# A Gauss elimination beside a matrix exponential: new step, filled pauses, another order of loads

## The chip, the cores and the metric

The kernel runs on one core of a Trainium2 chip. The metric is device time in microseconds. Three runs of the kernel before took 2057.63, 2059.76 and 2062.48 us; their median, 2059.76, is the time before. A profile is one more execution: it took 2060.89 us, of which the trace spans 2059.2.

## The reference, cut to what matters

The input x has 8 batches of 512 tokens of 576 features. It is first rotated in a subspace of 64 dimensions, and then goes through one transformer block (layer norm, modulation, attention of 16 heads over the heads of each token, a projection, a wide layer and back).

```
U, _ = qr(P)                       # P is 576 x 64
v = silu(cond) @ W.T + b           # 2016 entries for each batch
A[iu, ju] = v; A[ju, iu] = -v
R = expm(A)                        # 64 x 64 for each batch
z = x @ U
x = x + (z @ R - z) @ U.T
ada = silu(cond) @ ada_w + ada_b   # shifts, scales and gates of the block
x = x + gate * attention(modulate(layernorm(x)))
x = x + gate * mlp(modulate(layernorm(x)))
```

So before the first token can enter the block, the kernel needs U (64 columns made orthogonal, with the signs that a Householder QR gives them), the exponential for that batch, and the shifts and scales.

## The kernel before, in words

**Two parts.** Everything up to L568 is the preparation, inside one block in which the order on four engines (PE, DVE, ACT, POOL) is the order in which the program writes the instructions; SP, which issues the loads, is ordered by a scheduler, which may also put later loads early. An engine takes its instructions in that order, so one that waits holds all behind it. After L568 comes the main part: 16 units of 256 tokens. Its opening (L1045 to L1098) is written out by hand: `rotation(b)` is a list of six pieces (`project_z` of each half, `rotate` of each tile of 128 tokens, L591 to L638), `feature_major` (L640) turns normed tokens and applies the shifts and scales, `qkv` (L671) makes six groups of 288 columns for one tile, ten matmul passes each, and `attention` (L700) runs on DVE. `next_sums` (L905) makes sums of weights on POOL.

**The Gauss steps.** The orthogonal basis comes from gram = P^T P (L271 to L274) by elimination. The tile w is 128 x 130. Rows 0 to 63 hold gram and beside it an identity; rows 64 to 127 hold the first 64 rows of P, from which the signs are found. `pivot(j)` (L276 to L315) is run 64 times. PE spreads row j over 64 partitions by a product with a column of the identity, four times: two halves of `row`, two of `own` (L283). DVE finds the sign of the leading element of the lower half (L294), adds half the scaled own row with that sign (q, L295), inverts q's first element (r, L300), makes one factor for each row (co, L301, with `below`, which is -1 under the diagonal and 0 above), and updates the window of w by one multiply-add (L304). ACT takes the root of the own leading element (hd, L308), DVE inverts it (inv, L309), and ACT scales the own row for the next step's q (rows2, L310). The next step's spreads read w.

**Beside the steps.** After each pivot, `next(side)` (L482) runs one piece of `beside` (L462): first the entries of A (`skew_entries`, five chunks of 4 concurrent column tiles of 504 columns, from the weights wr, 1 MB a chunk), which go to memory and come back in another layout (au), then the exponential (`expm`, a polynomial and 19 squarings of all eight matrices, each 16 passes of 64 x 64 on PE and one multiply-add on DVE), and three rounds of the modulation's weights (`ada_round`). At steps 48 to 52 the first 128 tokens are multiplied by P (L487).

**The tail, L495 to L568.** The scaled basis (mps, mn), one correction of its orthogonality (ups, u1, g2, fix, fps), the result m2; then ut (U in rows, L538), gz (rotation minus identity times U, L553), u (U in columns, ups2) and the rotation of the first 128 tokens from px: first_zT, first_rot (L563). Then their norm (L568), feature_major and the first group of qkv (L684).

Here is what the diff does to a step's core, before:

```
nc.vector.tensor_scalar(signs[:, j : j + 1], row[:, 0:1], 0.0, 0.5, ALU.is_ge, ALU.subtract)
nc.vector.scalar_tensor_tensor(q, rows2[j % 2][:, j : j + WIN], signs[:, j : j + 1], row, ALU.mult, ALU.add)
nc.vector.reciprocal(r[p], q[p, 0:1])
nc.vector.scalar_tensor_tensor(co[p], w[p, j : j + 1], r[p], below[p, j : j + 1], ALU.mult, ALU.mult)
```

Of the kernel before, what the change touches and what calls it, by code (L numbers as in the profile page):

```python
# [18 lines left out]
R = 64  # L19
# [30 lines left out]
def rotate_then_dit_block(  # L50
# [113 lines left out]
    with tc.manual_schedule(engines=engines), tc.tile_pool(name="prep", bufs=1) as prep, tc.tile_pool(  # L164
# [3 lines left out]
    ) as ps_row, tc.tile_pool(name="ps_g", bufs=2, space=PSUM) as ps_g, tc.tile_pool(  # L168
# [8 lines left out]
        nc.gpsimd.memset(w, 0.0)  # L177
        load_rows(ct, cond_t, 64)
        load_rows(m, p_in, 64)
        nc.sync.dma_start(out=w[R:128, 1 : R + 1], in_=p_in[0:R])  # L180
        nc.sync.dma_start(out=pt, in_=p_t)
# [11 lines left out]
        nc.gpsimd.tensor_copy(w[0:R, R : 2 * R], ident[0:R, 0:R])  # L193

        below = prep.tile([128, WIN], F32, tag="below", name="below")
        nc.gpsimd.memset(below, -1.0)
# [14 lines left out]
        inv = prep.tile([128, R], F32, tag="inv", name="inv")  # L211
# [18 lines left out]
        load_ada(0, (0,))  # L230

# [28 lines left out]
        nc.gpsimd.tensor_scalar(is_, i1, SIN_C[3], None, ALU.mult)  # L260
        tri = prep.tile([R, R], F32, tag="tri", name="tri")
# [7 lines left out]
        first_xt = xin.tile([128, D], F32, tag="xt", name="xt_0_0", bufs=2)  # L269
# [6 lines left out]
        def pivot(j):  # L276

            p = slice(0, R) if j == 0 else slice(0, 128)
            row = ps_row.tile([128, WIN], F32, tag="row", name=f"row_{j}")
            own = ps_g.tile([128, R], F32, tag="own", name=f"own_{j}")  # L280

            def spread(out_, k, rhs):
                nc.tensor.matmul(out_, lhsT=ident[:, k : k + 1].to_broadcast([128, R]), rhs=rhs, start=True, stop=True)  # L283

            if j:
                spread(row[R:128], j + R - 1, w[:, j : j + WIN])
            spread(row[0:R], j, w[:, j : j + WIN])
            for h in range(2):
                spread(own[h * R : h * R + R, 0 : R - j], j, w[:, j:R])
            q = step.tile([128, WIN], F32, tag="q", name=f"q_{j}")  # L290
            r = step.tile([128, 1], F32, tag="r", name=f"r_{j}")
            co = step.tile([128, 1], F32, tag="co", name=f"co_{j}")
            if j:
                nc.vector.tensor_scalar(signs[:, j : j + 1], row[:, 0:1], 0.0, 0.5, ALU.is_ge, ALU.subtract)  # L294
                nc.vector.scalar_tensor_tensor(  # L295
                    q, rows2[j % 2][:, j : j + WIN], signs[:, j : j + 1], row, ALU.mult, ALU.add
                )
            else:
                nc.vector.tensor_copy(q[p], row[p])
            nc.vector.reciprocal(r[p], q[p, 0:1])  # L300
            nc.vector.scalar_tensor_tensor(  # L301
                co[p], w[p, j : j + 1], r[p], below[p, j : j + 1], ALU.mult, ALU.mult
            )
            nc.vector.scalar_tensor_tensor(  # L304
                w[p, j + 1 : j + WIN], q[p, 1:WIN], co[p], w[p, j + 1 : j + WIN], ALU.mult, ALU.add
            )
            hd = step.tile([128, 1], F32, tag="hd", name=f"hd_{j}")
            nc.scalar.activation(hd, own[:, 0:1], AF.Sqrt, scale=0.25)  # L308
            nc.vector.reciprocal(inv[:, j : j + 1], hd)  # L309
            nc.scalar.activation(  # L310
                rows2[(j + 1) % 2][R:128, j + 1 : R + 1],
                own[R:128, 0 : R - j],
                AF.Identity,
                scale=inv[R:128, j : j + 1],
            )  # L315
# [15 lines left out]
        def skew_entries():  # L331
            n = NSKEW // 4
            ps = ps_m.tile([128, n], F32, tag="m", name="skew_ps")
            for c in range(NK):
                column_tiles(ps, wr, c, [t * n for t in range(4)], n)
                if c == NK - 1:
# [13 lines left out]
                yield  # L350
                yield

        def ada_round(g):
            ps = ps_m.tile([128, 320], F32, tag="m", name=f"ada_{g}")
            for c in range(NK):
                column_tiles(ps, aws[g], c, [0, 256, D, D + 256], 320)
                if c < NK - 1:
                    yield
            rows = prep.tile([128, 320], F32, tag=f"ada_rows{g}", name=f"ada_rows_{g}")
            nc.scalar.copy(rows, ps)  # L360
            if g == 0:
                load_ada(2)
                nc.sync.dma_start(out=first_xT, in_=x_t[0, :, :, 0:256].rearrange("c p s -> p c s"))
                nc.sync.dma_start(out=first_xt, in_=x[0, 0:128, :])
                nc.sync.dma_start(out=b1, in_=fc1_b)
# [4 lines left out]
            yield  # L370
# [16 lines left out]
            yield  # L387
# [11 lines left out]

        def expm():  # L400
# [3 lines left out]
            yield True  # L404
            nc.vector.tensor_tensor(a, au, products(au, i1, "at"), ALU.subtract)
            yield True
# [9 lines left out]
            yield True  # L416
            nc.scalar.copy(s2, products(s1, s1, "ss"))
            multiply_add(hc, s1, COS_C[4], ic)
            yield True
            nc.scalar.copy(s3, products(s1, s2, "sss"))  # L420
            multiply_add(hs, s1, SIN_C[4], is_)
            yield True
            multiply_add(hc, s2, COS_C[5], hc)
            yield False
            ps = products(s3, hc, "hc")
            multiply_add(hs, s2, SIN_C[5], hs)
            yield True
            ps2 = products(s3, hs, "hs")
            nc.vector.tensor_tensor(even, even, ps, ALU.add)
            yield True  # L430
            multiply_add(odd, s1, SIN_C[1], i1)
            yield False
# [6 lines left out]
            yield False  # L439
            nc.vector.tensor_tensor(odd, odd, ps2, ALU.add)  # L440
            yield False
            ps = products(a, odd, "sn")
            multiply_add(even, s2, COS_C[2], even)
            yield True
# [3 lines left out]
            yield False  # L448
            for k in range(N_SQUARINGS):
                e, f, e_next, f_next = es[k % 2], fs[k % 2], es[(k + 1) % 2], fs[(k + 1) % 2]  # L450
                if k < N_SQUARINGS - 1:
                    multiply_add(e_next, e, 2.0, products(f, e, f"pe_{k}"))
                    yield True
                multiply_add(f_next, f, 2.0, products(e, f, f"pf_{k}"))
                yield True
            nc.vector.tensor_tensor(fmi, f_next, nan.unsqueeze(2).to_broadcast([128, B // 2, R]), ALU.add)
# [5 lines left out]
        def beside():  # L462
            yield
            yield from skew_entries()
            yield
            yield
            yield
            rest = chained(ada_round(g) for g in range(3))
            for k, busy in enumerate(expm()):
                if not busy or k in (0, 2, 4):  # L470
                    next(rest, None)
                elif k > 16:
                    next(rest, None)
                yield
            for _ in rest:
                yield

        side = beside()
        xps = None
        for j in range(R):  # L480
            pivot(j)
            next(side, None)  # L482
            if 48 <= j < 48 + NK:
                c = j - 48
                if c == 0:
                    xps = ps_m.tile([R, 128], F32, tag="m", name="xps")
                nc.tensor.matmul(xps, lhsT=m[0 : KROWS[c], c], rhs=first_xT[0 : KROWS[c], c, 0:128], start=c == 0, stop=c == NK - 1)  # L487
                if c == NK - 1:
                    px = prep.tile([R, 128], F32, tag="px", name="px")
                    nc.scalar.copy(px, xps)  # L490

# [4 lines left out]
        diag, mt, mn = square("diag"), square("mt"), square("mn")  # L496
        nc.vector.scalar_tensor_tensor(diag, inv[0:R], 0.5, ident[0:R, 0:R], ALU.mult, ALU.mult)
        row = ps_row.tile([128, WIN], F32, tag="row", name="row_64")
        nc.tensor.matmul(row[:, 0:1], lhsT=one_row.to_broadcast([128, 128]), rhs=w[:, R : R + 1], start=True, stop=True)
        mps = ps_g.tile([R, R], F32, tag="own", name="mps")  # L500
        nc.tensor.matmul(mps, lhsT=w[0:R, R : 2 * R], rhs=diag, start=True, stop=True)
        nps = ps_g.tile([R, R], F32, tag="own", name="nps")
        nc.tensor.matmul(nps, lhsT=diag, rhs=w[0:R, R : 2 * R], start=True, stop=True)
        nc.vector.tensor_scalar(signs[:, R : R + 1], row[:, 0:1], 0.0, 0.5, ALU.is_ge, ALU.subtract)
        nc.scalar.copy(mn, mps)
# [4 lines left out]
        def u_rows(ps, of):  # L510
            for c, rows in enumerate(KROWS):
# [3 lines left out]
        sps = ps_row.tile([R, R], F32, tag="row", name="sps")  # L515
        nc.tensor.matmul(sps, lhsT=one_row.to_broadcast([128, R]), rhs=signs[:, 1:WIN], start=True, stop=True)
        nc.scalar.copy(u1[:, 0:4], ups[:, 0:4])
        nc.scalar.copy(u1[0:R, 4], ups[0:R, 4])
        upper, level, fix = square("upper"), square("level"), square("fix")
# [8 lines left out]
        fps = ps_g.tile([R, R], F32, tag="own", name="fps")  # L528
        nc.tensor.matmul(fps, lhsT=mt, rhs=fix, start=True, stop=True)
        nc.scalar.copy(m2, fps.unsqueeze(1).to_broadcast([R, 2, R]))  # L530
        for _ in side:
            pass
        first_zT = prep.tile([R, 128], F32, tag="first_zT", name="first_zT")
        zps = ps_row.tile([R, 128], F32, tag="row", name="first_z")
        nc.tensor.matmul(zps, lhsT=m2[:, 0], rhs=px, start=True, stop=True)
        for n in range(2):
            ps = ps_ex.tile([128, HALF], F32, tag="ex", name=f"ut_{n}")
            nc.tensor.matmul(  # L538
                ps,
                lhsT=m2.rearrange("p h i -> p (h i)"),  # L540
                rhs=pt[:, n * HALF : (n + 1) * HALF],
                start=True,
                stop=True,
            )
            if n == 0:
                nc.scalar.copy(ut[:, 0:HALF], ps)
                nc.vector.tensor_copy(first_zT, zps)
            else:
                nc.vector.tensor_copy(ut[:, HALF:D], ps)
        for n in range(2):  # L550
# [3 lines left out]
            if n == 0:  # L554
                nc.scalar.copy(gz[0:R, cols], ps)
            else:
                nc.vector.tensor_copy(gz[0:R, cols], ps)
        ups = ps_m.tile([128, NK, R], F32, tag="m", name="ups2")
        u_rows(ups, m2[:, 0])
        for n in range(2):  # L560
            cols = slice(n * HALF, (n + 1) * HALF)
            ps = ps_ex.tile([128, HALF], F32, tag="ex", name=f"first_rot_{n}")
            nc.tensor.matmul(ps, lhsT=first_zT, rhs=gz[0:R, cols], start=True, stop=True)  # L563
# [645 lines left out]
```

## Time and profile before

| what | value |
|---|---|
| time, median of 3 runs | 2059.76 us |
| the profiled execution | 2060.89 us |
| its span in the trace | 2059.2 us |
| PE (TensorE products) busy | 1977.0 us, 96% |
| DVE (VectorE) busy | 1720.2 us, 84% |
| POOL (GpSimd) busy | 670.1 us, 33% |
| ACT (ScalarE) busy | 413.9 us, 20% |
| first spread of step 0 | 11.93 us |
| spread of the tail's first product (L499) | 139.16 us |
| first group of qkv | 161.38 us |

How to read it: the page cuts the span into 40 slices of 51.5 us and gives the busy share of each in tenths; the granted clock of PE stands in a row of its own. The timeline lists instructions by start: start, duration, engine, line, operation, what is written and read, shape, count, and in brackets how long the engine had been idle before it and what it waited for. A table by windows gives for each stretch the busy time (and the number of instructions) of PE, PE's weight loads, DVE, ACT and POOL, then the granted clock, the DMA share and its rate.

### The profile page before, as it was taken

The numbers are of one execution on the slowest core, as the hardware profiler recorded it, in microseconds if no ns is written. First come the engines' busy times: TensorE is split into PE (matmuls) and PEld (weight loads), VectorE is DVE, ScalarE is ACT, GpSimd is POOL, SyncE is SP. The second block draws the span as 40 slices with busy tenths as digits, with TensorE's granted clock in tenths as the row PEclk, the third lists the DMA queues.
The fourth block names the chain that finished last, engine by engine and source line by source line (L and its number), as shares of the span: only waits on it lengthen the run. The fifth ranks groups of instructions, "written<-read, shape, count | busy, mean of one in ns | idle before, by whom it ended". The sixth has DMA issues, their size and how long they took to land.

```text
span 2059.2 us, 27728 instructions
## 1 busy us (share of the span) xinstructions
PE 1977.0 (96%) x10314; PEld 1578.2 (77%) x10314; DVE 1720.2 (84%) x1874; ACT 413.9 (20%) x986; POOL 670.1 (33%) x883
## 2 busy tenths in 40 slices
PE   5889999999999999999999999999999999998998
PEld 2577678777788887878788787878787878886877
DVE  4756999999969889797969889797979998899921
ACT  2222222121211122121212222121212121121210
POOL 1003414334242333333232333323233444352422
PEclk7758999999999999999999999999999999999999
DMA  7315655849385765748386665758476757666664
GB/s 261 126 36 187 209 144 163 245 138 274 120 243 191 194 215 164 249 138 278 122 233 201 191 218 153 255 144 269 132 231 203 213 188 195 221 196 183 194 178 133
DMA packets 248126, 392.57 MB, mean 191 GB/s; under 512 B 86960, under 2 KB 131696, under 8 KB 247992
## 3 DMA queue, kind: packets, MB, share of 16 engines
q1 hardware_dynamic: 222072, 364.25, 58.8%
q10 hardware_dynamic: 25920, 26.55, 3.8%
q8 instruction: 81, 1.33, 0.3%
q14 instruction: 53, 0.43, 0.1%
HBM read 331.79 MB, written 58.94 MB: 190 GB/s over the span
## 4 chain that ended last, share of the span: by engine, by line
PE 74%; DVE 14%; issue 4%; DMA 3%; POOL 3%; ACT 1%; ACTq 0%; DVEq 0%; POOLq 0%; SPq 0%
PE fc L866 24%; PE qkvp L684 16%; PE fc L940 9%; PE pj L822 6%; PE fc L945 6%; PE fc L942 3%; PE p L971 3%; DVE sc L729 3%; DVE qk L722 2%; DVE att L759 2%; DMA w<-in_fc_w 2%; DVE pv L752 2%; PE row L283 1%; PE rot L625 1%; PE htr L657 1%
## 5 line engine op out<-in xcount | busy, mean ns | idle before, releaser
L866 PE MATMUL fc<-h2T,w 128*128 128x256 f32 x2304 | 518.4, 380 | 6.2 <-ACT h2T L842 3.4
L866 PEld LDWEIGHTS fc<-h2T,w 128*128 128x128 f32 x2304 | 431.5, 190 | 75.1 <-ACT h2T L842 10.7
L684 PE MATMUL qkvp<-wqkv,hT 128*128 128x288 f32 (+1 forms) x1920 | 481.8, 408 | 3.9 <-ACT qs L695 1.6
L684 PEld LDWEIGHTS qkvp<-wqkv,hT 128*128 128x128 f32 (+1 forms) x1920 | 362.1, 191 | 105.4 <-ACT qs L695 2.7
L722 DVE TENSOR_TENSOR qk<-qkv 128x2304 f32<-128x2304 f32 x128 | 336.9, 2632 | 4.3 <-ACT qkv L692 2.0
L752 DVE TENSOR_TENSOR pv<-sc,qkv 128x2304 f32<-128x2304 f32 x128 | 331.9, 2593 | 2.8
L759 DVE TENSOR_REDUCE att<-pv 128x144 f32<-128x2304 f32 x128 | 325.9, 2546 | 3.3
L729 DVE TENSOR_REDUCE sc<-qk 128x64 f32<-128x2304 f32 x128 | 326.0, 2547 | 2.5
L965 POOL TENSOR_TENSOR s<-gt 128x128 f32<-128x128 f32 x144 | 88.2, 614 | 468.2 <-ACT gt L887 468.2
L887 ACT ACTIVATE gt<-fc,b 128x256 f32<-128x256 f32 x288 | 118.7, 471 | 593.9 <-PE fc L866 560.3
L940 PE MATMUL fc<-wq,gt 128*128 128x288 f32 x576 | 170.8, 417 | 10.6 <-ACT gt L887 7.5
L945 PEld LDWEIGHTS fc<-wt,ss 128*128 128x128 f32 x1152 | 161.2, 191 | 15.3
L945 PE MATMUL fc<-wt,ss 128*128 128x144 f32 x1152 | 165.2, 287 | 0.0
L962 POOL TENSOR_TENSOR ss<-gt 128x128 f32<-128x128 f32 x144 | 124.6, 866 | 67.9 <-PE fc L945 67.9
L898 POOL TENSOR_TENSOR x<-x,mt 128x288 f32<-128x288 f32 x64 | 71.4, 1118 | 220.8 <-DVE mt L897 220.8
L695 ACT COPY qs<-qkvp 128x288 f32<-128x288 f32 x180 | 71.5, 397 | 352.1 <-PE qkvp L684 324.7
L940 PEld LDWEIGHTS fc<-wq,gt 128*128 128x128 f32 x576 | 99.4, 189 | 45.3 <-issue 15.9
L964 POOL TENSOR_TENSOR ss<-gt,ss 128x128 f32<-128x128 f32 x144 | 114.4, 794 | 10.0
L822 PE MATMUL pj<-w2q_p,aT 128*128 128x288 f32 x384 | 105.4, 411 | 7.9 <-DVE u L996 4.5
L147 POOL TENSOR_TENSOR rstd_m<-rstd_m,mhalf 128x1 f32<-128x1 f32 x32 | 24.5, 765 | 221.3 <-DVE rstd_m L146 221.3
L940 PE MATMUL fc<-wt,gt 128*128 128x288 f32 x288 | 94.0, 408 | 0.0
L942 PE MATMUL fc<-wq,ss 128*128 128x288 f32 x288 | 93.9, 408 | 0.0
(236 smaller groups left out, 2044.3 us busy)
## 6 DMA issues: line engine op xcount, KB each, us to landing
w<-in_fc_w SPq DMA_DIRECT2D x288, 256.0 KB, 4.8
wq<-in_fc_q SPq DMA_DIRECT2D x144, 432.0 KB, 4.9
wt<-comb_d SPq DMA_DIRECT2D x144, 432.0 KB, 5.5
tok<-qs ACTq DMA_DIRECT2D x180, 144.0 KB, 1.8
qkv<-tok SPq DMA_DIRECT2D x30, 864.0 KB, 4.6
w2q_p<-in_proj_w SPq DMA_DIRECT2D x32, 432.0 KB, 4.7
xT<-in_x_t SPq DMA_DIRECT2D x16, 640.0 KB, 4.5
w1t<-in_fc_t SPq DMA_DIRECT2D x80, 128.0 KB, 4.4
```

Source lines behind the costliest of these rows:

```text
L684: nc.tensor.matmul(ps, lhsT=hT[0:k, c, i * 128 : (i + 1) * 128], rhs=wqkv[0:k, c, cols], start=c == 0, stop=c == NK - 1,)
L722: nc.vector.tensor_tensor(pr, q[:, c * HC : (c + 1) * HC].unsqueeze(2).to_broadcast([128, HC, H, DH]), k.unsqueeze(1).to_broadcast([128, H ...
L729: nc.vector.tensor_reduce(sc[t][:, c * HC : (c + 1) * HC, :], pr, AX.X, ALU.add)
L752: nc.vector.tensor_tensor(pr, sc[t][:, c * HC : (c + 1) * HC, :].unsqueeze(2).to_broadcast([128, HC, DH, H]), v.unsqueeze(1).to_broadcast( ...
L759: nc.vector.tensor_reduce(att[:, c * HC : (c + 1) * HC, :], pr, AX.X, ALU.add)
L822: nc.tensor.matmul(ps, lhsT=aT[0:k, c, :], rhs=w, start=c == 0, stop=c == NK - 1)
L866: nc.tensor.matmul(bank[:, k], lhsT=lhs, rhs=h2T[rows, c, 0 : NU * 128], start=start, stop=stop, skip_group_check=True)
L887: nc.scalar.activation(gt[:, k].rearrange("p t s -> p (t s)"), bank[:, k], AF.Gelu, bias=b1[:, 2 * g + k : 2 * g + k + 1])
L940: nc.tensor.matmul(p[k], lhsT=whole[k][0], rhs=whole[k][1], start=g == 0, stop=stop)
L942: nc.tensor.matmul(p[2], lhsT=whole[2][0], rhs=whole[2][1], start=g == 0, stop=stop)
L945: nc.tensor.matmul(bank[:, side], lhsT=lhs, rhs=rhs[:, n * QUARTER : (n + 1) * QUARTER], start=False, stop=stop, skip_group_check=True,)
L962: nc.gpsimd.tensor_tensor(ss[:, 0], gt[:, 0, 1], gt[:, 1, 1], ALU.add)
```

## The change

It has four parts, all in the preparation and the opening.

*The step.* q's first element is the row's first element plus half the scaled own element, with one sign; in absolute value it is the sum of two absolute values. The row is now written beside a column that holds the second of them, so that one reduction over two columns (den) gives the denominator. r is taken from den, not from q, and the sign goes into co. `below` is -2, and the product of w's column with it (pend) is made at the end of the step before. PE spreads own once, not twice, and doubled. The root that goes into that column is ACT's; its reciprocal (inv) stands ahead of the update of w. ACT keeps the roots of the diagonal for the end (roots). The last step makes diag.

```
-            row = ps_row.tile([128, WIN], F32, tag="row", name=f"row_{j}")
-            own = ps_g.tile([128, R], F32, tag="own", name=f"own_{j}")
+            line, after = lines[j % 2], lines[(j + 1) % 2][:, 0:1]
+            row = line[:, 1 : 1 + WIN]
...
+            if not last:
+                own = ps_g.tile([128, R], F32, tag="own", name=f"own_{j}")
+                spread(own[R:128, 0 : R - j], j, w[:, j:R], twice)
+                nc.scalar.activation(after[R:128], own[R:128, 0:1], AF.Sqrt, scale=0.5)
+            nc.scalar.activation(roots[:, j : j + 1], row[0:R, 0:1], AF.Sqrt)
...
+            nc.vector.tensor_reduce(den[p], line[p, 0:2], AX.X, ALU.add, apply_absolute_value=True)
+            nc.vector.tensor_scalar(signs[p, j : j + 1], row[p, 0:1], 0.0, 0.5, ALU.is_ge, ALU.subtract)
+            nc.vector.reciprocal(r[p], den[p])
+            nc.vector.scalar_tensor_tensor(
+                q[p], rows2[j % 2][p, j : j + WIN], signs[p, j : j + 1], row[p], ALU.mult, ALU.add
+            )
+            if last:
+                nc.vector.reciprocal(roots, roots)
+                nc.vector.tensor_tensor(diag, roots, ident[0:R, 0:R], ALU.mult)
+            nc.vector.scalar_tensor_tensor(co[p], pend[p], r[p], signs[p, j : j + 1], ALU.mult, ALU.mult)
+            if not last:
+                inv = column("inv")
+                nc.vector.reciprocal(inv, after)
+                nc.scalar.activation(
+                    rows2[(j + 1) % 2][R:128, j + 1 : R + 1], own[R:128, 0 : R - j], AF.Identity, scale=inv[R:128]
+                )
             nc.vector.scalar_tensor_tensor(
                 w[p, j + 1 : j + WIN], q[p, 1:WIN], co[p], w[p, j + 1 : j + WIN], ALU.mult, ALU.add
             )
...
+            pend = column("pend")
+            nc.vector.tensor_tensor(pend, w[:, j + 1 : j + 2], below[:, j + 1 : j + 2], ALU.mult)
```

*Unread products.* Each piece of `beside` now says how long PE works for it, and after it PE gets a product of a constant tile (wide, set by POOL after is_) into a bank that nobody reads, as long as 0.9 us less that time.

```
+        def stream(us):
+
+            n = min(512, int((us - 0.05) * 600) // 32 * 32)
+            if n > 0:
+                nc.tensor.matmul(fill[:, 0:n], lhsT=ident, rhs=wide[:, 0:n], start=True, stop=True)
...
         for j in range(R):
-            pivot(j)
-            next(side, None)
+            pend = pivot(j, pend)
+            if j == R - 1:
+                break
+            busy = next(side, 0.0)
...
+            stream(0.9 - busy)
```

The pieces are spaced anew: skew's chunks stand in steps 1, 3, 5, 6 and 7, seven empty pieces follow, and the exponential starts at step 15; its last two products (of 19 squarings) come behind the loop, inside the tail. Modulation products share a step with the exponential from its piece 5 on, in pieces 5, 8, 9, 10 and from 12.

*Loads.* SP joins the engines whose order is the program's. P's rows are loaded first, and w's lower rows and the condition from ACT's queue; wr comes after the write of skew_ends; the second half of the first modulation weights comes after the loads of au.

```
-    with tc.manual_schedule(engines=engines), ...
+    with tc.manual_schedule(engines=engines | {mybir.EngineType.SP}), ...
...
-        nc.gpsimd.memset(w, 0.0)
-        load_rows(ct, cond_t, 64)
         load_rows(m, p_in, 64)
-        nc.sync.dma_start(out=w[R:128, 1 : R + 1], in_=p_in[0:R])
-        nc.sync.dma_start(out=pt, in_=p_t)
+        nc.scalar.dma_start(out=w[R:128, 1 : R + 1], in_=p_in[0:R])
+        nc.scalar.dma_start(out=ct[:, 0:4], in_=cond_t[0:512].rearrange("(c p) n -> p c n", p=128))
+        nc.scalar.dma_start(out=ct[0:64, 4], in_=cond_t[512:D])
```

*The first two tiles by z alone.* The first 256 tokens, not 128, are multiplied by P at steps 48 to 52. Of the exponential, the first batch also gets its transposed difference (first_back, 64 x 64). With it the rotated z of both tiles is made directly (zs, rps, zr), and both tiles are rotated in the preparation from ut; gz and u come behind them. `first[0]` and `first[2]`, the projection and the rotation of the second tile, are gone from the opening, and its norm comes after the first feature_major.

```
+        zps = lines[0][0:R, 0:256]
+        nc.tensor.matmul(zps, lhsT=m2[:, 0], rhs=px, start=True, stop=True)
+        nc.vector.tensor_copy(zs, zps)
...
+        ut_half(0)
+        rps = lines[1][0:R, 0:256]
+        nc.tensor.matmul(rps, lhsT=first_back, rhs=zs, start=True, stop=True)
+        nc.vector.tensor_copy(zr, rps)
+        ut_half(1)
...
+        def first_rotation(t, n):
+            cols = slice(n * HALF, (n + 1) * HALF)
+            pool, tag = ((ps_ex, "ex"), (ps_m, "m"))[t]
+            ps = pool.tile([128, HALF], F32, tag=tag, name=f"first_rot_{t}_{n}")
+            nc.tensor.matmul(ps, lhsT=zr[:, t * 128 : (t + 1) * 128], rhs=ut[0:R, cols], start=True, stop=True)
+            nc.vector.tensor_tensor(first_xt[t][:, cols], first_xt[t][:, cols], ps, ALU.add)
+
+        for t in range(2):
+            for n in range(2):
+                first_rotation(t, n)
+            if t == 0:
+                normed_x[0, 0] = [normed(first_xt[0], "a0_0")]
+            nc.sync.dma_start(out=xr_d[0][t * 128 : (t + 1) * 128, :], in_=first_xt[t])
+        ups = ps_m.tile([128, NK, R], F32, tag="m", name="ups2")
+        u_rows(ups, m2[:, 0])
```

In the first feature_major DVE makes every second chunk that ACT made before, and the first tile's groups of qkv come as 2, 3, 0, 1, and then 4, 5:

```
-    first[0]()
     feature_major(0, 0)
+    normed_x[0, 0] = [normed(first_xt[1], "a0_1")]
     q = qkv(0, 0)
-    now(q[:2])
+    now(q[2:4] + q[:2])
     next_sums()
-    first[2]()
-    now(q[2:4])
     first[3]()
     now(q[4:])
```

## The prediction

> **What bounds the kernel now.** I read the page's 40 slices first, then the busy time and granted clock by windows of 3.4 us over the first 190 us, then the timeline of the Gauss steps, the start and the tail, and last the waits of PE. Of the page, PE's busy tenths and its granted clock:
> ```profile
> PE   5889999999999999999999999999999999998998
> ...
> PEclk7758999999999999999999999999999999999999
> ```
> From the fourth slice on PE is full and its clock whole; the page gives it 1977.0 us of 2059.2. Ahead of that lie some 160 us at a low clock. The diff touches little else, so the question is when PE reaches the first product of qkv (161.38 us); from there on its own work sets the time, and I carry a gain at that point through one for one. Between 160 and 320 us the longest wait of PE is 1.4 us, which is the ground for that.
>
> One Gauss step, from the timeline (start, duration, what):
> ```profile
> 19.86 0.34 PE L283 MATMUL row<-w,ident 128*64 128x65 f32 x4 [0.39 <-DVE w L304]
> ...
> 20.25 0.16 DVE L294 TENSOR_SCALAR signs<-row 128x1 f32<-128x1 f32 x1 [0.36 <-PE row L283]
> 20.42 0.17 ACT L308 ACTIVATE hd<-own 128x1 f32<-128x1 f32 x1 [0.20 <-PE own L283]
> 20.51 0.28 DVE L295 SCALAR_TENSOR_TENSOR q<-rows,signs,row 128x65 f32<-128x65 f32 x1
> 20.82 0.16 DVE L300 RECIPROCAL r<-q 128x1 f32<-128x1 f32 x1
> 21.02 0.22 DVE L301 SCALAR_TENSOR_TENSOR co<-w,r,below 128x1 f32<-128x1 f32 x1
> 21.35 0.28 DVE L304 SCALAR_TENSOR_TENSOR w<-q,co,w 128x64 f32<-128x64 f32 x1
> 21.55 0.15 DVE L309 RECIPROCAL inv<-hd 128x1 f32<-128x1 f32 x1
> 21.68 0.20 PEld L283 LDWEIGHTS row<-w,ident 128*64 128x64 f32 x4 [1.51 <-DVE w L304]
> ```
> It is a ring: row, signs, q, r, co, w, row. By starts: row to signs 0.39, signs to q 0.26, q to r 0.31, r to co 0.20, co to w 0.33, w to the next row 0.33: 1.82 us. At the half clock the row takes 0.49 instead of 0.34 and the ring 1.97 (rows at 36.19, 38.17, 40.15). Two figures for later: inv, which depends on nothing near, starts 0.20 after w; ex_f starts 0.07 after a one-column inv (133.09 to 133.17). So a one-column instruction holds VectorE for 0.07 and one of 65 columns for 0.20, unless somebody needs the result.
>
> The clock, by windows (PE busy, PEld, DVE, ACT, POOL, then granted clock):
> ```profile
> 89.40:92.80 3.40, 3.21 (x64) 1.79 (x60) 2.84 (x13) 0.85 (x4) 0.00 (x0) 1.00 0.00 0
> ...
> 96.20:99.60 3.40, 2.10 (x48) 1.67 (x48) 2.75 (x13) 0.86 (x4) 0.00 (x0) 0.88 0.00 0
> 99.60:103.00 3.40, 2.94 (x46) 2.67 (x47) 2.59 (x13) 0.89 (x4) 0.00 (x0) 0.50 0.00 0
> ...
> 109.80:113.20 3.40, 3.40 (x51) 3.12 (x50) 2.47 (x12) 0.78 (x4) 0.00 (x0) 0.50 0.00 0
> 113.20:116.60 3.40, 3.40 (x56) 2.96 (x53) 2.55 (x13) 0.88 (x4) 0.00 (x0) 0.61 0.03 7
> ```
> At 94% busy the clock stays whole, at 62% it is lost, at the half clock 86% doesn't bring it back, and two windows without a pause do.
>
> **The change, part by part.** Sums are against the profiled execution (2060.89 us, span 2059.2); the median of the runs shown is 2059.76, 1.1 less.
>
> A. *Start to step 8, now 27.81 us.* Now the first row starts at 11.93, with w's 16 KB landing 6.9 us after its issue, behind two loads of wr. Loaded first, as ct is now (issued 0.80, used 2.81), gram and step 0 could run at about 5.5. But step 0 now ends in an unread product that reads wide, and wide is set by POOL after is_:
> ```profile
> 9.48 0.85 POOL L260 TENSOR_SCALAR ex_is<-ex_i 128x256 f32<-128x256 f32 x1
> 10.38 0.14 POOL L262 MEMSET tri<- 64x64 f32 x1
> ```
> POOL has one more small operation ahead (twice, 0.3 like L266) and two more memsets. The memset of 128x512 lies between 0.36 (128x320) and 0.58 (64x576). It ends near 11.2, and PE, in order, stands before it. The product has 480 columns in two passes: skew's four concurrent 504s take 1.91 at the half clock, so 1.8. Step 1 then starts at 13.2 instead of 13.60; the early load is nearly lost. Steps 1 to 7: skew's products stand in steps 1, 3, 5, 6, 7; PE is never idle, so the clock rises within some 5 us; 2.5 + 2.2 + 5 x 1.6 gives step 8 near 25.8: **-2.0**. SP is now in program order, so wr waits for skew_ends (POOL, 5.2) and is issued 2 us later; chunk 1 lands (7.2 after issue) at 13.0, needed at 13.7. If that cover is gone, each late microsecond is one. ACT issues three loads (0.5 each) ahead of silu; nobody needs it before 7.
>
> B. *Steps 8 to 63, 55 rings in 27.81 to 137.19, 1.99 each.* New ring: row to den 0.39; signs follows 0.07 behind; q needs signs, 0.26 more; r lies between them, because it needs den alone; co needs r and signs, both done, and starts 0.20 after q; w 0.33 after co; next row 0.33. Sum 0.39 + 0.07 + 0.26 + 0.20 + 0.33 + 0.33 = 1.58. pend starts 0.31 after w, beside PE's 0.33 + 0.39. den has no row of its own: below 0.07 it can't be, and its nearest kin, a reduction from 256 columns, has 0.40, like any 256-column operation, so 0.07 (the one-column rows) against 0.40; I take 0.07. inv now stands ahead of w, so w waits for ACT's root: root starts 0.56 after the row and takes 0.17, inv can start 0.98 after the row, 0.25 of slack. Some ten steps in which ACT still copies for the exponential (0.37 to 0.5 each) may exceed it by 0.2: +2.0. The exponential's multiply-add (0.40) ends about when den is due: up to 0.07 a step. A whole-clock step with pf and ada fills 88.81 to 90.53 of PE, so those fourteen cost 1.72 less a spread, plus its start, near 1.7. Seven fill-only steps at 1.58, 34 at 1.65, 14 at 1.72: 91.3. Against 109.4, **-18.1**, and +2.0.
> The fill: 288 columns take 0.25 a pass at the whole clock (5.02 for 20), so 480 take 0.84 in two; three spreads 0.4; 1.25 of 1.58, 79%, beside 0.3 of pause. At the half clock it is 0.6 + 1.8 and PE has no pause, which brings the clock back.
> [...]
>
> C. *Step 63 to mps, 137.19 to 139.71.* The last step takes a reciprocal of 64 columns (0.24 for 16, 0.16 for one: 0.5) and diag ahead of w, +0.67; row_64 goes behind mps, hd and the exponential behind it too. 2.25 against 2.52: **-0.3**.
>
> D. *mps to qkvp, 139.71 to 161.38, all at clock 0.50.*
> ```profile
> 146.17 0.68 PE L535 MATMUL first_z<-px,m 64*64 64x128 f32 x2 [0.35 <-ACT m L530]
> ...
> 161.38 7.45 PEld L684 LDWEIGHTS qkvp<-wqkv,hT 128*128 128x128 f32 x20 [1.80 <-issue]
> ```
> Up to first_z (6.46) PE now also does the last two products of the exponential (0.61 each). At the whole clock ups takes 1.2 for 2.4, g 0.8 for 1.5: 5.4. After first_z (15.2): z by first_back, no gz ahead of the rotation. first_z 0.45, ut 0.5, rps 0.45, copies 0.4 each, two products: second xt add 3.25 after first_z; stats to xn 2.9 as now, at 6.15. Then the new wait: ups2 takes the slot of the first product of tile 1, whose add stands behind xn on VectorE; u_rows start at 6.65, then g twice with a copy between (ps_g is one deep), htr at 9.5, hT split over two engines 2.2: 11.7. Together 17.1 for 21.7, **-4.6**. At the half clock it would be 8.4 + 14.2.
>
> E. *rotate(1) leaves the path between the groups of qkv*: rot 1.13, **-1.1**. xT for half 1 is free earlier; that hides nothing.
>
> Sum: -2.0 - 18.1 + 2.0 - 0.3 - 4.6 - 1.1 = -24.1. From the median, **2035.7 us**.
>
> **Rivals.** *The clock swings.* 79% lies between the 62% that lost it and the 94% that held it. Half the steps at 0.6 + 1.8 = 2.2 on average make the mean 1.9: 14 us less gained, 2049. *The ring doesn't shorten*: if den costs its whole 0.16 and 0.10 of scalar wait before q and co, it is 1.82 and the gain of B is 8 to 10: 2045. *The early load and the tail pay more*: the first step not held by wide, or the clock whole through the first qkv groups (7.88 for 20 at 161.4 against 5.02: 2.9): 2029. *The tail falls cold* inside: 5.5 less, 2041, in the forecast's own range. *Slower: the fill holds PE without ever bringing the clock up.* Place: each stream behind the spreads; price: 2.2 a step, 55 x 2.2 = 121 against 109, with a tail of 22.6 for 21.7, together +10: 2070. It decides if PE without a pause for over two windows stays at 0.50. 109.8 to 116.6 speaks against it. *It doesn't do what it says*: SP's order delays a load so that PE stands and the fill can't help: 2055.
>
> **How the numbers follow.** Forecast with the cold tail 0.53, swinging clock 0.16, ring 0.12, more 0.11, no effect 0.04 (three quarters of it within 0.2%), slower 0.04. The range reaches from a little beyond 2029 to a little beyond 2049: 2025 to 2051. Less than 0.2% (4 us) can't be told from none: faster 0.93, same 0.03, slower 0.04.
>
> **What would show it.** Ring 1.58 between rows in fill-only steps, clock 1.00 from 20 us to the tail; first fill released by POOL wide near 11; PE's wait for VectorE ahead of ups2 near 2.5 us; first qkvp near 136. Wrong it is if rings stay at 1.8, if the clock shows 0.50 among the steps, or if qkvp comes 25 us earlier and the end doesn't.

## The result, and the profile after

The changed kernel takes **2071.42 us** (median of 4 runs, 2070.41 to 2073.24), the kernel before, beside it, 2060.88 (2057.63 to 2062.48). The ratio is 1.0054, interval 1.0037 to 1.0072: **slower by 10.5 us**, where 2035.7 was forecast and faster had a chance of 0.93. The profiled execution took 2071.95 us, its span 2070.2.

The two rows of the page that were shown of before, now of the changed kernel:
```profile
PE   6889899999999999999999999999999999998998
...
PEclk9968999999999999999999999999999999999999
```
The first two slices of the clock went from 7 and 7 to 9 and 9: the unread products did what they were put in for. The third and fourth (5 and 8, now 6 and 8) hardly moved. So the loss is not a clock that never came up. It stands in the steps themselves. This is one step of the changed kernel, from the timeline; the ring of before is in the prediction:
```profile
20.67 0.34 PE L298 MATMUL line<-w,ident 128*64 128x65 f32 x4 [0.63 <-ACT rows L327]
...
21.12 0.15 ACT L306 ACTIVATE line<-own 64x1 f32<-64x1 f32 x1 [0.56 <-PE own L298]
21.29 0.16 ACT L307 ACTIVATE roots<-line 64x1 f32<-64x1 f32 x1
21.49 0.16 DVE L314 TENSOR_REDUCE den<-line 128x1 f32<-128x2 f32 x1 [0.77 <-ACT roots L307]
...
21.95 0.21 DVE L323 SCALAR_TENSOR_TENSOR co<-pend,r,signs 128x1 f32<-128x1 f32 x1
...
22.26 0.28 DVE L330 SCALAR_TENSOR_TENSOR w<-q,co,w 128x64 f32<-128x64 f32 x1
...
22.70 0.34 PE L298 MATMUL line<-w,ident 128*64 128x65 f32 x4 [0.61 <-ACT rows L327]
```
The bracket of den is the line to read: VectorE stood for 0.77 us, and what released it was ScalarE's `roots`, not TensorE's row. Row to den is 0.82 us; the forecast had 0.39. Den to co 0.46, co to w 0.31, w to the next row 0.44: together 2.03 at the whole clock, where before had 1.82. The list of waits of the changed kernel, 12 to 146 us, says that it is so in 62 of the 63 steps of that stretch (idle time in total, times, longest):
```profile
DVE den L314 <- ACT roots L307: 39.6, 62, 5.3
```
Nothing in the arithmetic makes den need the root. But both read the PSUM tile `line`, on two engines, and in the compiled program den waits on ScalarE's semaphore and starts within 0.04 us of the end of that very root.

The clock, by windows, from 110 us on (the columns are those of the prediction's windows):
```profile
110.00:120.00 10.00, 7.90 (x124) 5.19 (x124) 7.67 (x46) 3.27 (x16) 0.00 (x0) 1.00 0.01 2
120.00:125.00 5.00, 3.99 (x66) 3.20 (x65) 3.67 (x25) 1.47 (x8) 0.00 (x0) 0.90 0.41 134
125.00:130.00 5.00, 5.00 (x50) 4.05 (x50) 3.25 (x21) 1.19 (x7) 0.00 (x0) 0.50 0.00 0
```
It is whole until 124, with TensorE 79% busy, and then 0.50 until about 175, through the tail and the first groups of qkv, although from 125 to 140 TensorE is busy for 5.00 of every 5 us.

The start, and below it the tail, from the timeline (the prediction shows POOL's lines, first_z and qkvp of the kernel before):
```profile
11.10 0.53 POOL L270 MEMSET wide<- 128x512 f32 x1
...
11.68 1.97 PE L517 MATMUL fill<-wide,ident 128*128 128x480 f32 x2 [5.55 <-POOL wide L270]
...
153.22 1.11 PE L582 MATMUL line<-px,m 64*64 64x256 f32 x2 [0.35 <-ACT m L578]
...
164.73 2.37 PE L557 MATMUL ups<-m,pt 64*128 64x64 f32 x10
...
167.26 0.46 ACT L719 ACTIVATE hT<-htr,mod 128x128 f32<-128x128 f32 x1 [8.95 <-DMA xt<-in_x]
...
169.69 1.81 PE L742 MATMUL qkvp<-wqkv,hT 128*128 128x288 f32 x3
```
TensorE stood 5.55 us before the first unread product, and POOL's wide released it. In the tail hT's bracket names a DMA; but hT starts 0.16 us after the end of ups2 (164.73 + 2.37). This is a wait for several things of which the list names the wrong one; the experiment with ups2 early is for it.

| from the span's start, us | before | changed | roots behind q | all mends |
|---|---|---|---|---|
| row of step 1 | 13.60 | 13.58 | 13.62 | 10.61 |
| den (before: signs) of step 8 | 28.35 | 29.65 | 26.91 | 24.64 |
| mps | 139.71 | 145.22 | 122.02 | 119.66 |
| first z | 146.17 | 153.22 | 129.16 | 126.59 |
| first group of qkv | 161.4 | 169.69 | 145.64 | 144.38 |
| span | 2059.2 | 2070.2 | 2046.1 | 2042.0 |
| first group of qkv to the end | 1897.8 | 1900.5 | 1900.4 | 1897.6 |

### The profile page after: what moved, and what is told of

Read it like the earlier page. It is cut to its first block, busy times and chain, and to the rows that moved or that the text cites. A ratio compares the mean times of both kernels' runs of the same rounds, so it can differ in the third digit from the quotient of the medians.

```text
span 2070.2 us, 27820 instructions
## 1 busy us (share of the span) xinstructions
PE 1987.6 (96%) x10258; PEld 1577.2 (76%) x10258; DVE 1723.0 (83%) x2009; ACT 423.1 (20%) x1047; POOL 676.7 (33%) x887
## 4 chain that ended last, share of the span: by engine, by line
PE 77%; issue 8%; DVE 7%; DMA 4%; POOL 2%; ACT 2%; SPq 0%; ACTq 0%; POOLq 0%; DVEq 0%
PE fc L924 25%; PE qkvp L742 18%; PE fc L998 10%; PE pj L880 7%; PE fc L1003 6%; PE fc L1000 3%; PE p L1029 3%; DMA w<-in_fc_w 2%; DVE sc L787 1%; PE rot L673 1%; DVE pv L810 1%; DVE att L817 1%; PE htr L705 1%; DVE qk L780 1%; PE zps L662 1%
## 5 line engine op out<-in xcount | busy, mean ns | idle before, releaser
L147 POOL TENSOR_TENSOR rstd_a<-rstd_a,mhalf 128x1 f32<-128x1 f32 x32 | 22.1, 692 | 254.1 <-DVE rstd_a L146 254.1
L147 POOL TENSOR_TENSOR rstd_m<-rstd_m,mhalf 128x1 f32<-128x1 f32 x32 | 24.5, 765 | 219.2 <-DVE rstd_m L146 219.2
```

## The experiments

Times are medians, with the ratio to runs of the kernel before on the same chip. **Theory 1**: den waits for roots. **Rivals**: the unread products hold TensorE; den itself is slow; the early loads or the clock lose it.

**Roots behind q** (the changed kernel, one instruction moved; the last step keeps its place):
```
-            nc.scalar.activation(roots[:, j : j + 1], row[0:R, 0:1], AF.Sqrt)
             ...
             nc.vector.scalar_tensor_tensor(co[p], pend[p], r[p], signs[p, j : j + 1], ALU.mult, ALU.mult)
+            if not last:
+                nc.scalar.activation(roots[:, j : j + 1], row[0:R, 0:1], AF.Sqrt)
```


> In steps 0 to 62 ACT's root of the diagonal (roots) is issued behind q, and no longer ahead of den; all else is as in the changed kernel. Theory 1 (den stands behind roots because both read the same PSUM tile and the program puts roots first): den starts some 0.4 us after the row instead of 0.82, the ring of a fill-only step falls from 2.03 to about 1.62, step 63 starts some 20 us earlier (142.6 to about 122), and the time falls from 2071 to about 2050; lower, to 2040, if the shorter ring leaves PE so few pauses that the clock stays whole to the tail. Rival (what holds den is ACT's root into the column beside the row, or the queue of ACT itself): ring stays at 2.0 and the time at 2071.

2048.83, ratio 0.9937 (0.9921 to 0.9953): 22.6 us off (24 by the ratios) by moving one 0.16 us instruction that no step needs. A row, its den and the update of w:
```profile
46.43 0.34 PE L298 MATMUL line<-w,ident 128*64 128x65 f32 x4 [0.18 <-ACT rows L330]
...
46.80 0.16 DVE L315 TENSOR_REDUCE den<-line 128x1 f32<-128x2 f32 x1
...
47.64 0.29 DVE L333 SCALAR_TENSOR_TENSOR w<-q,co,w 128x64 f32<-128x64 f32 x1
```
Row to den is 0.37 us. The next row starts at 48.08, so this ring is 1.65. From den of step 8 to den of step 63 it takes 93.3 us, where the changed kernel takes 113.7.

**The changed kernel without the unread products:**
```
-            stream(0.9 - busy)
```


> The changed kernel without any unread product. Theory 1 (the slower step costs the change its gain, the fill keeps the clock in the first 120 us): the clock falls to 0.50 in most steps, a ring there takes 2.2 us instead of 2.03, step 63 starts 4 to 8 us later than with the fill, time 2073 to 2080. Rival (the fill itself delays the steps, as in the last 20 steps, 2.4 us each with PE never idle): time 2062 to 2068.

2079.74, 1.0088 (1.007 to 1.0105): 8.3 worse, 7 by the ratios. The unread products are not what made the change slower.

**The kernel before with the unread products alone** (wide, fill and stream put into it, 0.9 us less the work of each step):
```
+            if j < R - 1:
+                stream(0.9 - work[0])
```


> The kernel before with the unread products alone: after each step's piece PE gets a product of up to 480 columns, as long as 0.9 us less the estimated time of the piece (0.85 for a chunk of skew, 0.55 for a chunk of the modulation or a set of products, 0.4 for a turned set, 0.25 for a chunk of xps). Theory 1 (the fill is sound, the step of the change is what failed): clock 1.00 through the steps, ring 1.82 to 1.85 instead of 1.99 on average, step 63 starts 7 to 9 us earlier (137.2 to 129), time about 2052. Rival (the fill can't hold the clock beside the exponential, and costs when the clock is down): rings of 2.3 in part of the steps, time 2062 to 2070.

2054.56, 0.9969 (0.9953 to 0.9985): 6 better by the ratios. Its seven runs spread from 2049.7 to 2060.9, so the size is rough. In the profiled one the clock is at 1.00 from about 17 us to 133 but for 3.4 us.

**Roots read from another tile, in its place.** Moving the root changes two things, the order on ScalarE and the order of readers. So it was left where it is, and read from a column that one more product writes into own:
```
+            if not last:
+                spread(own[0:R, 0:1], j, w[:, j : j + 1])
-            nc.scalar.activation(roots[:, j : j + 1], row[0:R, 0:1], AF.Sqrt)
+            nc.scalar.activation(roots[:, j : j + 1], row[0:R, 0:1] if last else own[0:R, 0:1], AF.Sqrt)
```


> The changed kernel (2071.4) with roots left where it is in the order of issue, ahead of den, but read from a column that one more product writes into own, so that den's tile line has VectorE as its only reader. Theory 1 (den waits because ScalarE's root and den read one PSUM tile, and readers of one tile on two engines are put one behind the other): the row to den is 0.4 to 0.6 us again, the ring 1.65 to 1.75, and the kernel 2048 to 2053, like the one with roots behind q. Rival (it is the place of the root: ScalarE between after and rows, so that inv and rows are late, or den itself is slow): row to den or den to the next row stays long, ring near 2.0, 2066 to 2073.

2139.73, 1.0371 (1.0354 to 1.0388). Both theories missed it by over 66 us. Its timeline:
```profile
42.33 0.37 PE L298 MATMUL own<-w,ident 128*64 128x1 f32 x2 [0.24 <-ACT line L306]
42.63 1.97 PE L519 MATMUL fill<-wide,ident 128*128 128x480 f32 x2
```
The extra product waits for ScalarE, which reads own, and pushes the fill back; 480 columns take 1.97 us, as in the cold start, where the whole clock takes 1.07 (at 29.11 in the changed kernel). The ring is 3.1, TensorE is some 93% busy, and the clock first comes up near 220 us, in the tail. (The column PEclk reads 1.00 up to there: it has no record before the first change; the durations tell.) This is the mechanism of the prediction's slower rival, which I had not meant to make. It told only that den is now released by the row.

**The same, with the extra product ahead of own's**, so that TensorE doesn't wait for ScalarE:
```
+                spread(own[0:R, 0:1], j, w[:, j : j + 1])
                 spread(own[R:128, 0 : R - j], j, w[:, j:R], twice)
```


> As the kernel with roots read from own, but the extra one-column product stands ahead of own's product, so that TensorE never waits for ScalarE between a row and its fill. Roots still stands ahead of den in the order of issue. Theory 1 (the shared tile orders den behind the root; the slow run before was the half clock, which the extra pause of 0.24 us in each ring of 3.1 never let come up): the clock comes up near 18 us as in the others, row to den 0.4 to 0.6, ring 1.65 to 1.8, 2048 to 2055. Rival (the place of the root on ScalarE is what costs): ring near 2.0 at the whole clock, 2066 to 2073. If the clock stays at half again, 2100 and more, and the extra product itself would be the reason.

2050.46, 0.9947 (0.9931 to 0.9964), the clock up near 16 us, 94.4 us from den 8 to den 63:
```profile
41.19 0.34 PE L298 MATMUL line<-w,ident 128*64 128x65 f32 x4
...
41.57 0.16 DVE L315 TENSOR_REDUCE den<-line 128x1 f32<-128x2 f32 x1
...
41.89 0.17 ACT L308 ACTIVATE roots<-own 64x1 f32<-64x1 f32 x1
```
The root is still issued first and runs 0.32 us after den, and only in the last step, where it reads the row again, does it release den. The shared tile was the cause, not the root's place.

**Roots behind q, without the unread products** (the same line taken out):

> The roots-behind-q kernel without the unread products. In the changed kernel taking them out cost 8.3 us, in the kernel before putting them in gained 6. Theory A (the clock needs them just as much in the shorter ring): 2055 to 2058. Theory B (in a ring of 1.65 the other products already fill TensorE above the share that holds the clock): 2047 to 2051.

2057.29, 0.9977 (0.9967 to 0.9986): 8.5 worse than with them. In the short ring they are worth as much.

**Longer unread products in the changed kernel:**
```
-            stream(0.9 - busy)
+            stream(1.35 - busy)
```


> The changed kernel (2071.4) with each fill drawn up for 1.35 us of its ring of 2.03 instead of 0.9, up to 512 columns. Theory A (the clock fell at 124 because the last steps hold many short products of 64 rows and only 160 columns of fill in a ring of 2.03; what counts is streaming in full products, not TensorE being occupied): the clock stays 1.00 to the end of step 63, near 137, mps near 139 to 141 instead of 145.2; 2064 to 2068. Theory B (the stretch of the half clock comes whatever the fill is): 0.50 from about 124 again, and with longer fills a ring of 2.5 or more at the half clock; 2071 to 2076.

2071.44, 1.0044 (1.0027 to 1.006): no time gained. The clock half of theory A held, its time did not:
```profile
125.00:130.00 5.00, 4.76 (x65) 2.94 (x66) 3.62 (x21) 1.53 (x9) 0.00 (x0) 1.00 0.29 100
```
The same stretch had 0.50 in the changed kernel. But the longer products put the row back, by some 0.1 us in part of the steps, step 8 came 0.8 later, and mps came at 145.71.

**Fill in the last step and the tail** (on roots behind q; three shorter ones in the tail are left out here):
```
             if j == R - 1:
+                stream(0.9)
+                stream(0.7)
                 break
```


> The roots-behind-q kernel (2048.8) with two unread products of 480 and 384 columns put into TensorE's 2.2 us pause of the last step, and three short ones into the pauses of the tail. Theory A (the pause of the last step loses the clock: it goes to 0.50 near 124 us, and the tail and the first qkv groups run at half): the clock stays 1.00 past 125 us, mps to the first qkvp falls from 23.6 us to 18 to 20, some 2 us more in the first qkv groups; 2041 to 2043. Theory B (the clock falls there whatever TensorE does, as it fell at 124 in the changed kernel with TensorE 80% busy): still 0.50 from about 125, the added products only delay mps by up to 0.5 us; 2049 to 2051.

2047.45, 0.9929 (0.9916 to 0.9943), 1.6 better than roots behind q by the ratios. The two intervals overlap widely, and it lies between the two theories. In its profile mps to qkvp falls from 23.6 to 18.8 with the clock at 1.00 until 140; but a dip of 10.2 us among the early steps takes 4 of that back.

**wide and the loads early** (on roots behind q): wide is set behind rows2, and skew_ends is written behind wr:
```
-        nc.sync.dma_start(out=skew_d[:, 0 : VD : VD - 1], in_=skew_ends)
         ...
+        nc.sync.dma_start(out=skew_d[:, 0 : VD : VD - 1], in_=skew_ends)
         load_ada(0, (0,))
```


> The roots-behind-q kernel with wide set early on POOL and the write of skew_ends issued behind the loads of wr. Theory A (the early row was lost to POOL's wide at 11.68 and to wr's first chunk at 14.51, which stood on SP behind the write and nine hoisted loads): first fill near 8 to 9 us, step 1 at 9 to 10 instead of 13.6, step 8 some 4 us earlier; 2044 to 2046. Theory B (the loads share the DMA engines and wr lands no earlier, or the clock comes up later, so that skew's products take the gain): step 1 earlier but step 8 within 1 us of before; 2048 to 2049.

2046.44, 0.9928 (0.9914 to 0.9943): 1.9 better by the ratios, between the two theories, and again with overlapping intervals. In the profile the first fill starts at 6.50 instead of 11.72 and mps comes 3.6 earlier. Step 1 starts at 10.77, because ScalarE's second table load (1.28 us from 8.56) now holds inv until 10.26.

**ScalarE in order in the opening** (on roots behind q):
```
-    held.enter_context(tc.manual_schedule(engines={mybir.EngineType.PE, mybir.EngineType.Pool, mybir.EngineType.DVE}))
+    held.enter_context(tc.manual_schedule(engines=engines))
```


> The roots-behind-q kernel with ScalarE's instructions of the opening issued in the order of the program too, so that the first exp of the attention no longer stands ahead of qkv's copies and hT. Theory A (the 3.5 us that TensorE waits for ScalarE's qkv copy ahead of htr is on TensorE's path, which sets the opening): that wait falls below 1.5, from the first qkvp to the end 1897 instead of 1900.5; 2045 to 2046. Theory B (VectorE sets the opening and the wait is covered, or another copy is late in its place): no change, 2048 to 2050.

2044.33, 0.9915 (0.9901 to 0.9929): 4.5 better by the ratios, with intervals that just overlap. TensorE's longest waits from qkv's first groups to 330 us, first without and then with this order:
```profile
PE htr L708 <- ACT qkv L753: 3.5, 1, 3.5
```
```profile
PE zps L665 <- ACT gz L659: 1.7, 1, 1.7
```
The wait of 3.5 is gone, and one of 1.7 has come. From the first group of qkv to the end it now takes 1899.0, in a profiled execution that was the slowest of the six (2048.04).

**ups2 early** (on roots behind q): ups2 goes ahead of the first rotation, into own's bank, and the two g into lines[0] and lines[1]:
```
         ut_half(1)
+        ups = ps_g.tile([128, NK, R], F32, tag="own", name="ups2")
+        u_rows(ups, m2[:, 0])
```


> The roots-behind-q kernel with the product ups2 and its copies put ahead of the first rotation (in another PSUM tile), and the two products g in two PSUM tiles. Theory A (hT's first write waits for ups2, which is the last to read the memory that hT takes over, and not for the DMA that the list of waits names: it began 0.16 us after ups2's end): hT begins within 1 us of htr's end, near 141 instead of 143.2, and the first qkvp comes 1.5 to 3 us earlier; 2045.5 to 2047.5. Theory B (it waits for the store of tile 1): hT still at 143 or later; 2049 to 2050.

2048.54, 0.994 (0.9926 to 0.9954): nothing. hT now follows 1.3 us behind htr's start instead of 3.5, so the wait was ups2's; but htr itself comes 3.4 later: the first rotation starts 2.0 later, behind ups2, and both g now stand ahead of htr, which waits for ScalarE's copy of the second.

**All mends** (roots behind q, fill in the last step and tail, early wide and loads, ScalarE in order):

> The roots-behind-q kernel with the fill of the last step and tail, the early wide and loads, and ScalarE in order in the opening, together. Theory A (the losses stand one behind the other on one path: step 1 at 10, rings of 1.65, tail at the whole clock near 18.5, opening without the wait for ScalarE): 2048.8 less some 3 (loads), 3 to 5 (clock in the tail), 4.5 (ScalarE): 2036 to 2039, which is the forecast. Theory B (what comes earlier is given back, to a clock that falls for some 10 us in any stretch where TensorE is busy for about 80%, or to the transfers of the opening): 2041 to 2045.

**2040.29**, 0.9893 (0.9879 to 0.9908): faster than both kernels, between the two theories. By the ratios the parts (13.0, 1.6, 1.9 and 4.5) make 21.0 and the whole 22.1. That fits losses that stand one behind the other, but of the single parts only the first is clear of the noise.

**All mends with ups2 early**, a fill ahead of htr and hT on ScalarE alone:

> All mends, and ups2 with its copies ahead of the first rotation, both g in PSUM tiles of their own, an unread product in the pause before htr, and hT on ScalarE alone. Theory A (ups2 early gained nothing at the half clock because TensorE was always busy there; at the whole clock it goes into pauses): first_z to the first qkvp falls from 13.4 us in the kernel with the filled last step to 10 to 11; 2033 to 2036. Theory B (the tail is bound by its chain of copies and the order of TensorE only trades one wait for another): within 1 us of all mends without it.

2041.50, 0.9897 (0.9882 to 0.9912): no gain. The clock was lost near 122 all the same, and first z to qkvp took 17.7; the case that theory A speaks of did not come about.

**All mends with longer fills** (1.05 for 0.9, two more short ones behind mps and ups):

> All mends (2040.3), with each fill drawn up for 1.05 us instead of 0.9 and two more short products behind mps and ups, in the tail. Theory A (the clock is lost at mps because the tail's products have 64 rows; more full products around it hold it): 1.00 past 130, mps to the first qkvp 18 to 20 instead of 24.7; 2035 to 2038. Theory B (the fills in the tail stand ahead of products on the path, and the clock falls there anyway): 2040 to 2043.

2043.61, 0.9905 (0.9891 to 0.992): within the noise of all mends. Its profile holds the clock to about 129, and mps comes 1.3 later for it.

## Why the prediction was wrong

**A, the start (-2.0 forecast).** Wide held the first fill to 11.68 (near 11 was forecast), and step 1 came at 13.58 (13.2). So far right. Steps 1 to 7 then ran at the long ring, and step 8 came about 1 us later than before. With the roots mended it comes 1.3 earlier.

**B, the steps (-18.1 + 2.0).** This is the step that failed, in its first term: "row to den 0.39". I took it from row to signs of before, where VectorE alone waits for the row, and asked who produces what den reads, not who else reads it. It was 0.82. The 55 rings took 113.7 for a forecast of 93.3, and that is 20.4 of the miss; some 3 of it are the last rings, 2.40 each at the half clock, where those ahead of them took 1.99. With the roots moved they take 93.3, so the other terms of B were right in their sum (row to den 0.37 in that run; den to w 0.84 where 0.86 was forecast; w to the next row 0.43 where 0.33 was). Part of that is luck. In that run 44 of the 55 rings take 1.64 to 1.67, where 1.58 was forecast without work beside them: 3.9 us more in all. Against it, the 6.3 us set aside for the exponential, the modulation and ScalarE came to some 2.2. Of den's own price, the low end was right: signs starts 0.08 behind it.

**C, the last step (-0.3).** Step 63 to mps takes 2.63, before 2.52, forecast 2.25: the reciprocal of 64 columns and diag were priced rightly, the first wait again not.

**D, the tail (-4.6).** mps to qkvp took 24.5, forecast 17.1, and 22.6 if cold. It was cold; of the other 1.9, hT's wait for ups2 is a part. I had ups2 ahead of htr. In the program as compiled htr comes first, and hT waits for ups2's end. By my reading hT takes over memory that ups2 still reads; the run with ups2 early shows the wait, not its reason.

**E, the opening (-1.1).** The rotation of the second tile is gone, but from the first group of qkv to the end it became 2.7 longer: "I carry a gain through one for one" failed. The exp of the attention, issued on ScalarE ahead of one of qkv's copies, waits for VectorE, and TensorE waits 3.5 us for that copy:
```profile
210.19 0.42 ACT L794 ACTIVATE sc<-sc 128x256 f32<-128x256 f32 x1 [3.65 <-DVE sc L793]
210.51 0.38 ACT L750 COPY qkv<-qkvp 128x288 f32<-128x288 f32 x1
...
210.94 1.16 PE L705 MATMUL htr<-ident,xm 128*128 128x128 f32 x4 [3.50 <-ACT qkv L750]
```
With ScalarE in order this wait is gone. From the first group of qkv to the end, the profiles give back 1.4 of the 2.7 in that run, and all of it in all mends.

A, B, D and E miss by about 3.0, 20.5, 7.4 and 3.8 us, C by 0.4: 35.1 of the 35.2 us between the profiled run and the same sum set against the profiled run of before (2060.89 - 24.1).

**The rivals.** The swinging clock was the mechanism I feared most; it cost the last eight steps and the tail, not the steps before. What I held against the slower rival, that two windows without a pause bring the clock back, did not hold: from 125 to 140 us TensorE had no pause, and the clock stayed at 0.50. The rival nearest in kind was "the ring doesn't shorten", at 2045: it priced den's duration and not a wait, so it couldn't reach the other side. The slower rival gave 2070 by another way, which this kernel didn't go; the first run with roots from own shows that such a state exists.

**What stays open.** Why the clock falls in one profile and holds in another with the same fill in the last step (on roots behind q it held to 140, with all mends it fell near 122), and why a TensorE that is always busy with products of 64 rows, as from 125 to 140 in the changed kernel, doesn't bring it back. In seven profiles, the changed kernel's among them, the whole clock lasts the same 105.81 us, or 31 times 3.41, although it came up between 13.9 and 18.2 us and the steps end at 145 us in one and ahead of 123 in the others. Where it held to 140 it had come up anew at 37.5, and lasted 102.4 us. So the fall may hang on the time since the rise, and not only on what TensorE does there. Longer unread products made it last 129.7 us in the changed kernel and 112.6 in all mends; no run separates the two. Also open are why w to the next row takes 0.10 longer than before, and whether the chip needs the order of the two readers that the program keeps. The serial halves of hT, split over two engines on one tile, were seen (0.5 to 0.8 us apart), not measured by themselves.

## What to carry to other kernels

When a chain gets a new first operation, list every reader of the tile that it reads, on all engines, with the order of issue: a side result that no step needs can stand in a ring 62 times, and moving it here gave 22.6 us. Read the bracket of the first operation in a ring before any duration. A gain at the start of the next stage is carried through only if the engines outside the written order do there what they did before: here ScalarE, which is outside it, put one exp ahead of a copy that TensorE then waited 3.5 us for, and from the first group of qkv to the end it took 2.7 us longer.

## What the runs showed of the hardware

Unread products are worth 6 to 8.5 us here in three kernels, and what they are seen to change for the better is the granted clock. Without them it is lost four times in the steps of the kernel before (at 23.7, 57.8, 98.8 and 119.3 us), and from 23.7 to 47.6 it stays at 0.50 with no pause of TensorE over 1.3 us. In roots behind q without them the longest pause of TensorE between 30 and 126 us is 1.2 us, and the clock is lost four times: from 31.8, 61.5, 92.9 and 112.7 us on the spread of a row takes 0.43 to 0.49 us, and ahead of each 0.34.

In all 16 profiles each stretch at the half clock inside the span is a whole multiple of 3.41 us by the clock's records (the longest has 15 of them in the changed kernel, and 8 in eight other profiles). In the kernel before they last 23.89, 20.48, 17.07, 47.79 and twice 3.41 us, in the changed kernel 51.20, 6.83 and three times 3.41. That TensorE was busy did not bring the clock back in the changed kernel: from 125 to 140 it was busy for 5.00 of every 5 us, and the clock stayed at 0.50. With longer unread products (448 columns where there were 160) the same stretch kept 1.00, with TensorE busy for 4.76 to 4.88 of every 5 us.
